# A transformer block with adaptive layer norm: turning rotated queries and keys by DMA instead of TensorE in 22 of 32 tiles

## The chip, the cores and the metric

The kernel runs as one program on one core of a Trainium2 chip. The metric is the device time of one execution in microseconds; the kernel before takes 1667.65 us (median of three runs, 1667.3 to 1667.76). All data is float32 unless said otherwise. Engines are called as in the profile: PE is TensorE's matrix multiplication and PEld its weight load, DVE is VectorE, ACT is ScalarE, POOL is GpSimd, SP is SyncE, which issues most of the DMAs.

## What is computed

The input x has 2 batches of 2048 tokens with 256 features. Six vectors per batch (`sa` to `gb`) come from a small conditioning matrix. Cut to what matters:

```python
h = layernorm(x) * (1 + ca) + sa
k = apply_rope(h @ Wk.T); v = h @ Wv.T            # one key and value head of 128
q = apply_rope(einsum('btd,hkd->bhtk', h, Wq))    # two query heads of 128
scores = einsum('bhtk,bsk->bhts', q, k) * 128 ** -0.5     # causal
x = x + ga * (softmax(scores) @ v ... @ Wo.T)
h = layernorm(x) * (1 + cb) + sb
x = x + gb * ffn(h)         # 8 experts, 256 -> 1024 -> 256, each token weighed by a gate

# apply_rope, on pairs of neighbouring features:
out = stack([x0 * cos - x1 * sin, x1 * cos + x0 * sin], axis=-1)
```

The gate gives a token to those experts alone whose softmax weight lies above a threshold of its own, so the experts work on lists of tokens.

## The kernel before

It has two parts. The **attention part** (function `attention`) goes over 32 tiles of 128 tokens, 16 of each batch. The **experts' part** (function `experts`) then goes over the eight experts' lists in items of 256 tokens, in loops whose counts are read from the data; its two products are L1202 (h) and L1193 (y). It begins when the attention part has ended, at about 488 us.

The 32 tiles are taken in groups, four tiles of batch 0, four of batch 1 and so on, at the end in twos and ones. A tile's place in this sequence is its rank r, 0 to 31; tiles 8 to 11, for example, are tiles 4 to 7 of batch 0. The function `tile_steps` writes down the steps of one tile:

- Load x (L448, SP), moments (L423, L425 on DVE; L429, L430 on POOL), normalised rows xn (L459, DVE or POOL), their transposes on PE (L468), hT with scale and shift (L476, L478), and the projection to queries, keys and values (L489, PE, 128x512 in PSUM). ACT copies v (L495).
- The rotation: L505 multiplies queries and key by the cosines and L513, in two instructions, the swapped pairs by the signed sines (both DVE, out of PSUM into tiles t); L522 adds the two products, on DVE or POOL.
- The rotated tile is 128 tokens by 3 x 128 features. `turn_rot` transposes its three blocks on PE into PSUM (L529), and `qT_out` copies them out with ACT: the key's block into kT, which holds all keys of a batch (L532), the queries' two blocks into qT, times the scale 128^-0.5 (L534).
- The scores (L545, PE) against all keys so far, at most 512 at a time, a causal mask on the last block (L549); `keep` copies them to SBUF and takes their maximum (L556, DVE, with a product by 1.0); L563, exp on ACT (L572), transposes of the weights (L618), their copy (L622), product with v (L628), output projection (L662), sum with x (L669), store (L678).
- Second layer norm (L685, L688), a split of the float32 rows into 16-bit halves on POOL (L695) and their store to a list of features (L702), the gate (L710 to L727), and for each group of tiles the places in the experts' lists, which POOL scatters (L826).

After the last tile, PE does two items of the first expert ahead (L975, L992), whose tokens were gathered from the features, transposed by DMA as 16-bit halves (L918) and joined by DVE (L924).

The order of the work is settled when the program is built, by the class `Plan`. Each step is added with an engine or a choice of engines, a cost for each in microseconds, steps that it comes after, buffers that it takes and gives back (`room` holds how many of each there are), a rank, and `late`, the time until its result is there once its engine is free. `Plan.run` goes through time: of the steps that are ready, whose engine is free and whose buffers are there, it takes the one of lowest rank, on the first of its engines that is free. Each engine then runs its instructions in exactly this order; a change of a cost or of a buffer's room can change the order on all engines. On the chip an instruction waits for semaphores of what it depends on.

## Time and profile before

| What | us |
|---|---|
| median of three runs | 1667.65 |
| the profiled execution | 1669.28 |
| its span, from first to last instruction | 1667.5 |
| PE busy, whole span | 1621.9 |
| start of the experts' first product L1202 | 488.39 |
| PE busy, 60 to 175 us (115 us) | 112.18 |
| DVE busy, 60 to 175 us | 90.27 |
| PE busy, 175 to 400 us (225 us) | 224.00 |
| DVE busy, 175 to 400 us | 139.62 |

A line of a group gives the source line, engine, operation, what it writes and reads, shape and count; then its busy time in us and the mean of one in ns; then how long the engine was idle just before such instructions, and what ended that. The busy time of PE counts each matrix multiplication to its modelled end, though the next has begun by then, so neighbours overlap. A line of a timeline begins with start and length in us. A line of the table by stage gives the stretch, its length, and the busy time of each engine with its number of instructions, then the granted clock of PE, the share of the DMA engines and GB/s.

### The profile page before, as it was taken

What the parts mean: (1) busy time and instruction counts of PE and PEld (TensorE: products, weight loads), DVE (VectorE), ACT (ScalarE), POOL (GpSimd) and SP (SyncE); (2) the same over time, 40 slices, a digit from 0 to 9 for tenths busy, and PEclk for the clock granted to TensorE, in tenths of its full rate; (3) what the DMA queues carried; (4) which work ended last, traced back from release to release, by engine and by line L of the source; (5) the groups of instructions that cost most, each with busy time, mean ns of one, the idle gap of its engine ahead of it and who ended that gap; (6) DMA issues with size and microseconds to landing.
All of it is one profiled execution on the core that took longest, in us unless ns stands there. A gap on an engine that the chain in (4) does not pass through costs nothing.

```text
span 1667.5 us, 26732 instructions
## 1 busy us (share of the span) xinstructions
PE 1621.9 (97%) x7666; PEld 1349.4 (81%) x7666; DVE 660.7 (40%) x2144; ACT 582.1 (35%) x1417; POOL 912.0 (55%) x1032
## 2 busy tenths in 40 slices
PE   8999999999989999999999999999999999999997
PEld 5666776777778888888888888888888888888886
DVE  6987666566532222223322322232232222222322
ACT  3555655555522222222222222222222222222222
POOL 5565334231127767647756765675776477634443
PEclk9999999999999999999999999999999999999999
DMA  5411000010033353335335333533533333433333
GB/s 181 149 39 36 23 30 26 17 39 14 14 87 57 62 115 60 62 57 109 56 65 108 57 59 58 108 57 59 108 57 59 57 58 58 69 57 57 64 57 48
DMA packets 165949, 106.35 MB, mean 64 GB/s; under 512 B 111040, under 2 KB 157248, under 8 KB 165760
## 3 DMA queue, kind: packets, MB, share of 16 engines
q0 software_dynamic: 41968, 46.83, 17.6%
q1 hardware_dynamic: 116048, 46.22, 12.1%
q10 hardware_dynamic: 7872, 12.58, 2.4%
q8 instruction: 26, 0.43, 0.1%
q14 instruction: 35, 0.29, 0.1%
HBM read 50.39 MB, written 31.86 MB: 49 GB/s over the span
## 4 chain that ended last, share of the span: by engine, by line
PE 67%; issue 1%; DMA 1%; another core or an unknown queue 1%; POOL 1%; POOLq 0%; DVE 0%; ACT 0%; SPq 0%; DVEq 0%; ACTq 0%
PE y L1193 33%; PE h L1202 33%; DMA list<-entry,place 0%; POOL out L1352 0%; DMA out<-yo,who 0%; ACT g L1228 0%; DMA xp<-xr 0%; DMA xr<-feats,at 0%; POOL list L1342 0%; POOL out L1385 0%; POOLq L1143 0%; DVE xT L1256 0%; DVE yb L1280 0%; DVE yo L1295 0%
## 5 line engine op out<-in xcount | busy, mean ns | idle before, releaser
L1193 PE MATMUL y<-w,g 128*128 128x256 f32 x2640 | 658.2, 381 | 15.3 <-ACT g L1228 10.4
L1202 PE MATMUL h<-xT,w 128*128 128x256 f32 (+1 forms) x2752 | 659.6, 373 | 4.7 <-DVEq L1306 4.7
L1228 ACT ACTIVATE g<-h,b_sb 128x256 f32<-128x256 f32 (+1 forms) x688 | 317.9, 465 | 860.9 <-PE h L1202 744.2
L1202 PEld LDWEIGHTS h<-xT,w 128*128 128x128 f32 x2752 | 515.0, 192 | 74.8 <-DVEq L1306 5.1
L1193 PEld LDWEIGHTS y<-w,g 128*128 128x128 f32 x2640 | 498.6, 190 | 86.0 <-ACT g L1228 11.9
L1352 POOL DMA_INDIRECT out<-yo,who x172 | 282.2, 1641 | 231.2 <-DVE yo L1295 178.2
L1256 DVE COPY xT<-xp 128x512 uint16<-128x512 uint16 x172 | 68.4, 439 | 647.3 <-PE h L1202 522.8
L1342 POOL DMA_INDIRECT list<-new,to x216 | 227.7, 1054 | 93.6 <-issue 75.3
L1318 POOL DMA_INDIRECT xr<-feats,at x172 | 175.0, 1017 | 100.5 <-POOL at L1363 70.5
L545 PE MATMUL psc<-kT,qT 128*128 128x512 f32 (+3 forms) x320 | 143.4, 534 | 0.0
L628 PE MATMUL pav<-pT,v 128*128 128x256 f32 x544 | 142.6, 384 | 0.0
L556 DVE TENSOR_SCALAR_CACHE_REDUCE s<-psc 128x512 f32<-128x512 f32 (+3 forms) x160 | 95.3, 605 | 62.5 <-PE psc L545 48.2
L628 PEld LDWEIGHTS pav<-pT,v 128*128 128x128 f32 x544 | 96.0, 190 | 29.7 <-issue 20.1
L1280 DVE TENSOR_TENSOR yb<-y,b_bc 128x256 f32<-128x256 f32 x165 | 62.6, 420 | 138.2 <-PE y L1193 134.4
L572 ACT ACTIVATE s<-s,nmx 128x512 f32<-128x512 f32 (+3 forms) x160 | 103.9, 651 | 36.9 <-DVE nmx L563 36.4
L622 ACT COPY pT<-ptr 128x512 f32<-128x512 f32 (+1 forms) x144 | 76.6, 564 | 51.7 <-PE pav L628 33.2
L826 POOL DMA_INDIRECT list<-entry,place x40 | 42.6, 1066 | 74.2 <-DVE place L823 43.4
L1271 DVE SCALAR_TENSOR_TENSOR gate<-gb_bc,mcur,part 128x256 f32<-128x256 f32 x172 | 75.8, 482 | 3.0
L618 PEld LDWEIGHTS ptr<-ident,s 128*128 128x128 f32 x544 | 63.4, 142 | 14.3 <-ACT s L572 4.5
L618 PE MATMUL ptr<-ident,s 128*128 128x128 f32 x544 | 72.5, 274 | 2.1 <-ACT s L572 1.9
L429 POOL TENSOR_SCALAR rstdf<-mvf 128x1 f32<-128x1 f32 x32 | 8.7, 272 | 113.5 <-DVE mvf L425 86.1
L1363 POOL COPY at<-sheet 128x2 int32 x85 | 61.2, 720 | 10.5 <-DMA xp<-xr 10.5
(165 smaller groups left out, 1104.8 us busy)
## 6 DMA issues: line engine op xcount, KB each, us to landing
w<-in_w ACTq DMA_DIRECT2D x12, 1024.0 KB
x<-in_x SPq DMA_DIRECT2D x32, 128.0 KB, 2.1
out<-x SPq DMA_DIRECT2D x32, 128.0 KB, 1.7
feats<-hp SPq DMA_DIRECT2D x32, 128.0 KB, 1.7
w<-in_w SPq DMA_DIRECT2D x4, 1024.0 KB, 9.1
list<-new,to POOLq DMA_INDIRECT x216
xr<-feats,at POOLq DMA_INDIRECT x172
out<-yo,who POOLq DMA_INDIRECT x172
```

What stands on the lines that cost most here:

```text
L545: nc.tensor.matmul(ps[:, :w], st["qT"][:, h, :], kT[:, ds(c * SC, w)], start=True, stop=not last)
L556: nc.vector.tensor_scalar(s[:, :w], st["sc", h, c][:, :w], 1.0, None, ALU.mult, ALU.max, accum_out=st["mx", h][:, c : c + 1],)
L572: nc.scalar.activation(s[:, :w], s[:, :w], AF.Exp, bias=st["nmx", h], accum_out=st["den"][:, h, c : c + 1],)
L618: nc.tensor.transpose(ptr[:, j, h, :], s[:, ds((c0 + j) * P % SC, P)], ident)
L622: nc.scalar.copy(pT[:, :m], st["ptr", c0][:, :m])
L628: nc.tensor.matmul(st["pav"][:, : NH * P], v[:, c0 + j, :], st["pT", c0][:, j].rearrange("p h t -> p (h t)"), start=(c0 + j == 0), stop=(c ...
L1193: last = pe.matmul(ys[c], gs[f % 4][:, ts(c, P)], weights[e][1][:, f, :], start=(f == 0), stop=(f == NF - 1),)
L1202: last = pe.matmul(hs[f % 4][:, :w], weights[e][0][:, k, ts(f, P)], xT[:, k, :w], start=(k == 0), stop=(k == KD - 1),)
L1228: act.activation(gs[f % 4][:, :w], hs[f % 4][:, :w], AF.Gelu_apprx_tanh, bias=b1_sb[:, at : at + 1],).then_inc(sem["act"], 1)
L1318: pool.indirect_dma_start(out=xr[:, ts(c, 2 * D)], out_offset=None, in_=feats, in_offset=bass.IndirectOffsetOnAxis(ap=at[:, c : c + 1], ax ...
L1342: pool.indirect_dma_start(out=lists[e], out_offset=bass.IndirectOffsetOnAxis(ap=to[:, j : j + 1], axis=0), in_=new[:, j, :], in_offset=Non ...
L1352: pool.indirect_dma_start(out=rows, out_offset=bass.IndirectOffsetOnAxis(ap=who[:, c : c + 1], axis=0), in_=yo[:, c, :], in_offset=None, b ...
```

## The change

In tiles 8 to 29 the three transposes on PE and the two copies on ACT are replaced by three steps. `rot_halves` (POOL) splits the rotated tile, 128x384 float32, into its low and its high 16-bit halves, 128x768. `turn_rot_halves` (SP) transposes these six blocks of 128x128 with one DMA from SBUF to SBUF. `join_rot` (DVE, or POOL if DVE isn't free in the plan) interleaves the halves again, into kT and into qT, with two copies. Tiles 0 to 7, 30 and 31 go on as before. Since a join doesn't multiply, the scale moves from `qT_out` to `keep`, for all tiles.

The rotary table holds each cosine and sine once instead of twice (and the sines without sign): L505 reads each value twice by a step of zero, and of the two instructions of L513 the first becomes a product by -1 and by the table in one instruction. The four loads of the table are 256 KB each instead of 512. The tiles t get buffers of their own (`t0` and `t1`, three each, in place of the shared name `big`), the second of which also holds the halves; `rpT` has two. In the plan, the cost of xn on POOL goes from 0.65 to 1.3.

```diff
-    room = {"ps": 6, "pav": 2, "x": 9, "s": 16, "pT": 3, "hx": 4, "hp": 3, "qT": 3, "big": 3, "xn": 3,
-            "hT": 2, "hT2": 2, "aT": 2, "g_sb": 1, "sign": 1, "size": 1, "ga": 1}
+    room = {"ps": 6, "pav": 2, "x": 9, "s": 16, "pT": 3, "hx": 4, "hp": 3, "qT": 3, "t0": 3, "t1": 3, "xn": 3,
+            "hT": 2, "hT2": 2, "rpT": 2, "aT": 2, "g_sb": 1, "sign": 1, "size": 1, "ga": 1}
...
-    rope_sb = const.tile([P, NT, 2, HS], F32, name="rope_sb")
+    rope_sb = const.tile([P, NT, 2, HS // 2], F32, name="rope_sb")
...
-        n_n = add(["DVE", "POOL"], [0.42, 0.65], xn, [n_n], take=["xn"])
+        n_n = add(["DVE", "POOL"], [0.42, 1.3], xn, [n_n], take=["xn"])
...
             if z == 0:
-                src = src.rearrange("p (h f) -> p h f", h=3)
                 nc.vector.tensor_tensor(
-                    dst, src, table.unsqueeze(1).to_broadcast([P, 3, HS]), ALU.mult
+                    d4, src,
+                    table.unsqueeze(1).unsqueeze(3).to_broadcast([P, 3, HS // 2, 2]), ALU.mult,
                 )
             else:
...
-                for y in range(2):
-                    nc.vector.tensor_tensor(
-                        d4[:, :, :, y], src[:, :, :, 1 - y],
-                        t4[:, :, y].unsqueeze(1).to_broadcast([P, 3, HS // 2]), ALU.mult,
-                    )
-
-        n_r0 = add("DVE", 0.6, lambda: rot(0), [n_q, l_rope[i // 4]], take=["big"])
-        n_r1 = add("DVE", 0.75, lambda: rot(1), [n_q, n_v, n_r0], give=["ps"])
+                t3 = table.unsqueeze(1).to_broadcast([P, 3, HS // 2])
+                nc.vector.scalar_tensor_tensor(
+                    d4[:, :, :, 0], src[:, :, :, 1], -1.0, t3, ALU.mult, ALU.mult
+                )
+                nc.vector.tensor_tensor(d4[:, :, :, 1], src[:, :, :, 0], t3, ALU.mult)
+
+        n_r0 = add("DVE", 0.6, lambda: rot(0), [n_q, l_rope[i // 4]], take=["t0"])
+        n_r1 = add("DVE", 0.75, lambda: rot(1), [n_q, n_v, n_r0], take=["t1"], give=["ps"])
         n_r = add(
             ["DVE", "POOL"], [0.58, 1.0],
             lambda eng: of[eng].tensor_tensor(st["t", 0], st["t", 0], st["t", 1], ALU.add),
-            [n_r0, n_r1],
+            [n_r0, n_r1], give=["t1"],
         )
...
-            nc.scalar.mul(st["qT"].rearrange("p h t -> p (h t)"), st["pr"][:, : NH * P], scale)
-
-        n_t = add("PE", 0.48, turn_rot, [n_r], take=["ps"], give=["big"])
-        n_k = add("ACT", 0.65, qT_out, [n_t], take=["qT"], give=["ps"])
+            nc.scalar.copy(st["qT"].rearrange("p h t -> p (h t)"), st["pr"][:, : NH * P])
+
+        def rot_halves():
+            st["rp"] = work([P, 2, 3 * HS], "t1", "_h" + u, U16)
+            nc.gpsimd.tensor_copy(
+                st["rp"],
+                st["t", 0].rearrange("p h f -> p (h f)").bitcast(U16).rearrange(
+                    "p (f two) -> p two f", two=2
+                ),
+            )
+
+        def turn_rot_halves():
+            st["rpT"] = work([P, 2 * 3, P], "rpT", u, U16)
+            nc.sync.dma_start_transpose(st["rpT"], st["rp"].rearrange("p two f -> p (two f)"))
+
+        def join_rot(eng):
+            src = st["rpT"].rearrange("p (two h) t -> p h t two", two=2)
+            of[eng].tensor_copy(
+                kT[:, ts(i, P)].bitcast(U16).rearrange("p (t two) -> p t two", two=2),
+                src[:, 2],
+            )
+            st["qT"] = work([P, NH, P], "qT", u)
+            of[eng].tensor_copy(
+                st["qT"].bitcast(U16).rearrange("p h (t two) -> p h t two", two=2),
+                src[:, :NH],
+            )
+
+        if 8.0 <= r < NTOK // P - 2:
+
+            n_t = add("POOL", 0.95, rot_halves, [n_r], take=["t1"], give=["t0"])
+            n_t = add("SP", 1.3, turn_rot_halves, [n_t], late=2.2, take=["rpT"], give=["t1"])
+            n_k = add(
+                ["DVE", "POOL"], [0.75, 1.1], join_rot, [n_t], take=["qT"], give=["rpT"]
+            )
+        else:
+            n_t = add("PE", 0.48, turn_rot, [n_r], take=["ps"], give=["t0"])
+            n_k = add("ACT", 0.65, qT_out, [n_t], take=["qT"], give=["ps"])
...
-                s[:, :w], st["sc", h, c][:, :w], 1.0, None, ALU.mult, ALU.max,
+                s[:, :w], st["sc", h, c][:, :w], scale, None, ALU.mult, ALU.max,
...
-    cos, sin = np.cos(angles), np.sin(angles)
-    both = np.stack([cos, cos], axis=-1), np.stack([-sin, sin], axis=-1)
-    return np.concatenate([a.reshape(T, HS) for a in both], axis=1).astype(np.float32)
+    return np.concatenate([np.cos(angles), np.sin(angles)], axis=1).astype(np.float32)
```

More of the change, by code (lines that the diff above doesn't have):

```diff
@@ L294, in attention @@
         load(rope_sb[:, ds(4 * q, 4)], rope.rearrange("(q n p) (z f) -> p q n z f", p=P, n=4, z=2)[:, q],
-             512, rank=first if q == 0 else q * 8 - 7.5)
+             256, rank=first if q == 0 else q * 8 - 7.5)
         for q in range(NT // 4)
@@ L501, in rot @@
             table = rope_sb[:, i, z, :]
-            src = st["pq"][:, : 3 * HS]
+            src = st["pq"][:, : 3 * HS].rearrange("p (h j two) -> p h j two", h=3, two=2)
+            d4 = dst.rearrange("p h (j two) -> p h j two", two=2)
             if z == 0:
-                src = src.rearrange("p (h f) -> p h f", h=3)
                 nc.vector.tensor_tensor(
-                    dst, src, table.unsqueeze(1).to_broadcast([P, 3, HS]), ALU.mult
-                )
-            else:
-                src = src.rearrange("p (h j two) -> p h j two", h=3, two=2)
-                d4 = dst.rearrange("p h (j two) -> p h j two", two=2)
-                t4 = table.rearrange("p (j two) -> p j two", two=2)
-                for y in range(2):
-                    nc.vector.tensor_tensor(
-                        d4[:, :, :, y], src[:, :, :, 1 - y],
-                        t4[:, :, y].unsqueeze(1).to_broadcast([P, 3, HS // 2]), ALU.mult,
-                    )
-        n_r0 = add("DVE", 0.6, lambda: rot(0), [n_q, l_rope[i // 4]], take=["big"])
-        n_r1 = add("DVE", 0.75, lambda: rot(1), [n_q, n_v, n_r0], give=["ps"])
+                    d4, src,
+                    table.unsqueeze(1).unsqueeze(3).to_broadcast([P, 3, HS // 2, 2]), ALU.mult,
+                )
+            else:
+                t3 = table.unsqueeze(1).to_broadcast([P, 3, HS // 2])
[5 more added lines that the diff above has]
+        n_r1 = add("DVE", 0.75, lambda: rot(1), [n_q, n_v, n_r0], take=["t1"], give=["ps"])
         n_r = add(
```

## The prediction

> **What bounds the kernel now.** I read the page first (busy time, then the chain), then busy times by stage, the groups of instructions of the first 470 us, PE's waits, and PE's timeline around the transposes. The page:

> ```profile
> PE 1621.9 (97%) x7666; PEld 1349.4 (81%) x7666; DVE 660.7 (40%) x2144; ACT 582.1 (35%) x1417; POOL 912.0 (55%) x1032
> PE y L1193 33%; PE h L1202 33%; DMA list<-entry,place 0%; POOL out L1352 0%; DMA out<-yo,who 0%; ACT g L1228 0%; DMA xp<-xr 0%; DMA xr<-feats,at 0%; POOL list L1342 0%; POOL out L1385 0%; POOLq L1143 0%; DVE xT L1256 0%; DVE yb L1280 0%; DVE yo L1295 0%
> ```

> TensorE is busy all the time. The chain names only the experts (L1193, L1202), which start at 488 us and which the diff leaves alone: every microsecond that the attention part ends earlier moves them as a block. So the question is what bounds the part before. By stage (us, PE, PEld, DVE, ACT, POOL busy):

> ```profile
> 60.00:175.00 115.00, 112.18 (x555) 78.54 (x554) 90.27 (x343) 64.88 (x191) 69.49 (x100) 1.00 0.14 41
> 175.00:400.00 225.00, 224.00 (x1090) 160.41 (x1089) 139.62 (x520) 130.38 (x359) 69.07 (x96) 1.00 0.09 26
> ```

> In the second stretch PE has no spare time and DVE is at 62%. In the first PE is at 98%, but DVE at 78% is the runner-up (from 60 to 100 us it has 36.61 of 40 us). What the steps cost:

> ```profile
> L529 PE MATMUL pr<-ident,t 128*128 128x128 f32 x96 | 15.3, 275 | 2.6 <-POOL t L522 2.6
> ...
> L532 ACT COPY kT<-pr 128x128 f32<-128x128 f32 x32 | 8.5, 267 | 19.8 <-PE pr L529 19.1 <-PE pf L866 0.8
> ...
> L534 ACT ACTIVATE qT<-pr 128x256 f32<-128x256 f32 x32 | 12.6, 394 | 0.0
> ```

> 275 ns is not what a transpose takes from PE, since neighbours overlap. Its real price is the distance between starts:

> ```profile
> 405.02 3.25 PE L618 MATMUL ptr<-ident,s 128*128 128x128 f32 x28
> 408.11 1.03 PE L628 MATMUL pav<-pT,v 128*128 128x256 f32 x4
> ```

> 28 transposes of the same shape hold PE from 405.02 to 408.11: 0.110 us each, 0.33 us for the three of a tile.

> [...]

> **The change, part by part.**
> *PE.* In tiles 8 to 29 (22 tiles) three transposes go: 22 x 0.33 = 7.3 us of PE's own time. Tiles 8 to 17 have them before 175 us (3.3 us), tiles 18 to 29 after (4.0 us). With them goes a wait of PE for the rotated tile (POOL t L522), 1.8 us at 112 us; the other one (0.8 us at 57 us) is of an earlier tile and stays. What PE meets next without it are the features' transposes (L710, which wait for DVE, 1.4 us from 60 to 400 us).
> *ACT.* 22 x (0.267 + 0.394) = 14.5 us of copies go. ACT is at 57% there: worth nothing by itself. One PSUM buffer of six per tile goes too, which lets PE run further ahead; I count nothing.
> *POOL.* New: the split, 128x768 uint16. Nearest row: L695, 128x512 in 613 ns, so 613 x 768/512 = 0.92 us, 22 x 0.92 = 20 us. In the order in which the changed kernel issues, POOL also gets 13 of the 22 joins; a join is 256 + 512 elements, by the same row 0.31 + 0.61 = 0.92 us, 12 us; it loses 3 additions (1.01) and 5 of L459 (1.27), 9 us. Net +23 us, on an engine with 60% in the first stretch and 31% in the second: hidden.
> *DVE.* 9 joins: the same pattern as L924, 128x512 in 0.42 us, and half of that to all of it for the 256; I take 0.26: 0.68 x 9 = 6.1 us. Plus 3 additions (0.556) and 5 of L459 (0.47): 4.0 us. Net +10 us. The rotation's new form (one product by -1, the table repeated by a zero step) has the same elements; no row shows it. Ends: 0 to +0.1 us in each of 32 tiles; I take 0. The scale moves into L556, which multiplied by 1.0 before: nothing.
> *SP and the transfer.* 22 more issues. The row for it, of eight blocks where the new one has six:

> ```profile
> L918 SPq DMA_TRANSPOSE sign_p<-g_sb_r x2: 1231/1292/1352, 342.0 to 352.5; - x2
> ...
> DMA to landing us min/median/max: 3.0/3.1/3.1
> ```

> 22 x 1.29 = 28 us of SP's sequencer, mostly idle there; the landing is between 3.1 x 6/8 = 2.3 and 3.1 us, I take 3.1. Most new issues stand right behind a store of features (L702, waiting for POOL) and ahead of a store of results (L678, waiting for DVE); behind them wait loads of x, which run tiles ahead. DMA engines are at 9 to 14%.
> *Latency.* From the added tile to keys that can be scored it took 0.33 + 0.27 + 0.27 + 0.39, about 1.2 us. It will take 0.92 + 3.1 + 0.92 plus three handovers of 0.1, 5.2 us: 4 us more. The cover for that is the distance from a tile's projection to its first score. The tightest is tile 8:

> ```profile
> 62.67 1.88 PE L489 MATMUL pq<-wqkv_sb,hT 128*128 128x512 f32 x4
> ...
> 68.70 0.82 PE L529 MATMUL pr<-ident,t 128*128 128x128 f32 x6
> ...
> 74.89 1.02 PE L545 MATMUL psc<-kT,qT 128*128 128x512 f32 x2
> ```

> Its transposes start at 69.0 us, so 5.9 us lie between them and the score, 4.7 us spare. In the changed order the PE work between projection and score, added up with the pitches, is 12.6 us for tile 8, 13.0 and 13.7 us for tiles 14 and 15, 15 to 71 us for the others. So 4 us fit, barely in three tiles: a late landing there costs PE up to 2 us each. Tiles 30 and 31, with nothing behind them, stay on PE.
> *Order.* The planner deals all work anew. It draws projections and rotations forward (tile 31's by some 70 us), so about four more tiles' rotations (4 x 1.3 = 5 us of DVE), and most of the +10 us, fall before 175 us: DVE goes from 90 to about 102 of 115 us, 89%. There PE and DVE will stop each other more. Of the 3.3 + 1.8 us that go there I let 3.0 count; of the 4.0 us after, all.
> *Start.* The first part of the rotary table is 256 KB instead of 512 KB. PE's first wait is for another load (wm, 6.5 us), issued before it: nothing.

> Sum: 3.0 + 4.0 = 7.0 us. The profiled execution took 1669.3 us, its span 1667.5; it would become 1662.3 and 1660.5. The median of the runs is 1667.65, so I predict 1660.6.

> **The rivals.** *Everything counts* (chance 0.12): PE keeps all 7.3 + 1.8 us, and the freed PSUM buffers remove a few of the short gaps, 1 to 4 us: 1654 to 1658. For it: the larger distances. Against: DVE at 89%.
> *VectorE takes over before 175 us* (0.21): the gain there is lost and DVE's extra work pushes by up to 3 us; only the 4.0 us of the second stretch stay, 1663.7 to 1667. For it: 36.61 of 40 us at 60 to 100 us. Against: there its waits for scores (L556, 48.2 us in all to 460 us) still leave room.
> *Joins hold up their engines* (0.12), slower. Joins stand in DVE's and POOL's fixed order; behind one that waits for its landing stand the rstd of other tiles (L429, L430), then their normalised rows, then PE. If each of the 22 costs PE 0.6 us, that is 13.2 us against 7.0 gained: 1673.9. It decides above 0.32 us a tile on the mean. Against: the planner books 1.3 + 2.2 = 3.5 us for what I measure as at most 3.1, so joins should come after their landings.
> *It doesn't do what it says*: excluded; 30 instead of 96 transposes of rotated tiles are issued.

> **How the numbers follow.** The likeliest case has 0.55 (1658 to 1664), with the rivals 0.12, 0.21 and 0.12. A measurement of this kernel tells 0.2%, 3.3 us, from no change: faster is below 1664.3, slower above 1671.0. Faster: 0.55 + 0.12 + 0.03 of the VectorE case = 0.70; slower: 0.10; the rest 0.20. The range of 8 in 10 leaves out most of the slower case and the best of the better one: 1656 to 1668.5.

> **What would show it.** Right: the start of the experts' first long row of h (L1202, 488.39 us now) comes 7 us earlier; PE's time from 175 to 400 us falls by the pitch of the transposes, and PE waits for no join. Wrong: PE waiting for kT or qT in tiles 8, 14 and 15; DVE above 95% from 60 to 175 us; POOL's L429 waiting behind a join; landings above 3.5 us.

## The result, and the profile after

The changed kernel takes 1680.39 us (median of six runs, 1676.69 to 1685.88); the kernel before took 1667.7 us beside it (six runs, 1664.71 to 1673.84). The ratio is 1.0067, with an interval of 1.0048 to 1.0085: slower by 12.7 us, where 7 us less had been forecast. The profiled execution of the changed kernel took 1685.88 us, the longest of its six.

The attention part got shorter, as forecast, though by less. Its stages (us; busy time of PE, PEld, DVE, ACT, POOL, each with its count; then PE's clock, DMA share, GB/s) in the changed kernel:

```profile
60.00:175.00 115.00, 111.91 (x531) 77.00 (x530) 99.08 (x358) 61.53 (x173) 81.29 (x117) 1.00 0.25 63
175.00:400.00 225.00, 222.64 (x1065) 158.07 (x1064) 142.05 (x530) 127.36 (x340) 79.71 (x116) 1.00 0.14 35
```

DVE is at 99 us of 115 (90 before), POOL 22 us busier over both stretches, PE a little less busy. The new work, in the groups of instructions of the attention part and in the view of the tile `rpT`:

```profile
L536 POOL COPY t_h<-t 128x768 uint16<-128x768 uint16 x22 | 18.6, 847 | 4.3 <-DVE t L520 4.1
...
L554 POOL COPY qT<-rpT 128x512 uint16<-128x512 uint16 x13 | 9.0, 694 | 15.2 <-PE psc L580 10.6 <-PE pc L836 4.6
...
L549 POOL COPY kT<-rpT 128x256 uint16<-128x256 uint16 x13 | 5.4, 417 | 4.5 <-DMA rpT<-t_h 4.5
```

```profile
L545 SPq DMA_TRANSPOSE rpT<-t_h x22: 1210/1217/1682, 69.6 to 312.0; - x22
...
DMA to landing us min/median/max: 2.7/2.8/3.1
```

The split takes 0.85 us, a join 1.1 us on POOL, a landing 2.8 us. One figure in the second group matters later: POOL's joins stood still for 10.6 us until PE had read an older tile of queries. PE's waits in the attention part, after:

```profile
PE ph L741 <- DVE hx L719: 2.6, 6, 1.0
...
PE psc L576 <- POOL qT L554: 0.7, 1, 0.7
```

PE waits once for a join (0.7 us, at about 361 us), and more often than before for the features' rows (1.5 us in three waits there). Its last product of the attention part (`pya`) starts at 480.57 us, 2.78 us earlier than the 483.35 of before. PE's timeline at the seam (start, duration, line, idle before):

```profile
479.49 1.46 PE L1023 MATMUL pya<-w,s_g 128*128 128x256 f32 x6
486.47 3.74 PE L1233 MATMUL h<-xT,w 128*128 128x256 f32 x8 [5.52 <-issue]
```

So the experts start at 486.47 instead of 488.39 us. The wait at this seam grew by 0.85 us (before: 4.67 us, put down to DVE), so of the 2.78 us only 1.92 arrive there. From there to the end it takes 1196.8 us instead of 1179.1: the loss of 17.7 us lies wholly in a part that the diff doesn't touch, in which PE issues the same 5392 products. PE's waits in it, before and then after:

```profile
PE y L1193 <- ACT g L1228: 10.4, 8, 2.4
PE y L1193 <- issue: 4.6, 5, 2.1
PE y L1193 <- DVE yb L1280: 0.2, 1, 0.2
```

```profile
PE y L1224 <- ACT g L1259: 12.5, 15, 2.4
PE y L1224 <- issue: 6.9, 6, 2.2
PE h L1233 <- issue: 6.0, 4, 5.3
```

The last line is new. "issue" means that no semaphore explains the idle time. The longest case, in the timeline after:

```profile
1053.51 1.03 PE L1233 MATMUL h<-xT,w 128*128 128x256 f32 x4
1054.37 2.75 PE L1224 MATMUL y<-w,g 128*128 128x256 f32 x12
1054.97 0.38 ACTq L1268 DMA_DIRECT2D w<-in_w  x1
1062.45 3.78 PE L1233 MATMUL h<-xT,w 128*128 128x256 f32 x8 [5.32 <-issue]
```

It falls where PE goes from the fourth expert to the fifth: the line of ACT is the load of weights that ACT issues as it begins the fifth (L1268, one such load at the beginning of each of the first six experts). All that the next item waits for was there: the join of `xT` (L1287) was done at 1055.4 us, and the fifth expert's weights had been asked for at 763.9 us. This change of experts is a special one. The last item of an expert's list is a half item of 128 tokens if the list fills an odd number of 128-token tiles, and its code stands between the expert's loop and the next expert's. PE's products show a half item at the end of seven of the eight experts, as here at the third's (h is 128x128 instead of 128x256):

```profile
889.90 1.50 PE L1233 MATMUL h<-xT,w 128*128 128x128 f32 x12
```

The fourth expert alone has none, so there PE jumps over the half item's code. Behind the pause, eight products take 3.78 us, where four take 1.03 otherwise: the clock is halved (the granted clock is 0.50 from 1062.4 to 1066.3 us). The stretch of 1050 to 1080 us, before and then after:

```profile
1050.00:1080.00 30.00, 30.00 (x140) 26.21 (x139) 8.81 (x24) 7.43 (x16) 18.54 (x22) 1.00 0.58 124
```

```profile
1050.00:1080.00 30.00, 24.68 (x105) 21.05 (x104) 5.85 (x17) 5.60 (x12) 14.90 (x18) 0.89 0.54 115
```

140 products became 105. Over the whole experts' part, the distances between starts of PE's products exceed the usual 0.216 us by 40.5 us in sum after and 23.8 us before. Of that, products at halved clock account for 7.8 and 4.1 us, and pauses for the other 32.7 and 19.8 us. So 16.6 us of the 17.7 are explained, 12.9 by pauses and 3.7 by the clock. The pause at 1057 us and the slow products behind it are 7.7 us of this; the rest are shorter waits and the slow products behind them, of kinds that the kernel before has too; this execution is the longest of the six.

What was PE waiting for? The list of DMA queues has a kind that no line of the kernel issues; the page after, and the same list for the stretch from 1057 to 1062 us:

```profile
q8 instruction: 25, 0.41, 0.1%
```

```profile
q8 instruction: 1, 0.02, 1.3%
```

The times of these packets behind 484 us:

| kernel | PE's blocks of instructions, start in us |
|---|---|
| before | 602.6, 758.7, 894.2, 1054.6, 1176.0, 1342.1, 1547.3, 1648.2 |
| after | 491.3, **758.6, 792.7, 1059.6, 1091.8**, 1358.0, **1563.4, 1595.1**, 1685.2 |

Before, one comes with each of the seven half items, and one 2.8 us after the change from the fourth expert to the fifth. After, there are three pairs, 32 to 34 us apart (bold), and each stands across a change of experts, at 765, 1057 to 1062 and 1568 us: by that assumption the blocks' edges lie elsewhere in the experts' code. An expert's code of PE is 258 instructions long in the compiled program, nearly one such block, so an edge would fall at much the same point of every expert's code. The change took 135 instructions from PE ahead of this code (66 transposes are 132), and 44 copies from ACT. The place of an engine's loops is, in what follows, their position in the compiled program modulo 256, up to a constant that is the same for all kernels: 86 before and 207 after for PE, 81 and 37 for ACT. Where in this count a block begins isn't known; only the differences between places are used.

**Theory**: the change gains in the attention part what the traces show, and loses more because the loops of the experts' part slid to a bad place. **Rival**: the DMA transposes, or the smaller rotary table in memory, leave something behind that slows the experts.

### The profile page after: what moved, and what is told of

The parts are those of the page before. It is cut to its first block, busy times and chain, and to the rows that moved or that the text cites. A ratio compares the mean times of both kernels' runs of the same rounds, so it can differ in the third digit from the quotient of the medians.

```text
span 1683.3 us, 26660 instructions
## 1 busy us (share of the span) xinstructions
PE 1625.4 (97%) x7600; PEld 1348.3 (80%) x7600; DVE 665.3 (40%) x2169; ACT 572.8 (34%) x1374; POOL 931.2 (55%) x1072
## 4 chain that ended last, share of the span: by engine, by line
PE 68%; issue 1%; another core or an unknown queue 0%; ACT 0%; DMA 0%; POOLq 0%; DVE 0%; POOL 0%; DVEq 0%; ACTq 0%
PE h L1233 34%; PE y L1224 34%; ACT g L1259 0%; DMA out<-yo,who 0%; POOLq L1174 0%; DVE yo L1326 0%; DVE xT L955 0%; POOL out L1383 0%; DVE yb L1311 0%; DVEq L1523 0%; POOLq L1476 0%; POOLq L1383 0%; DVE who L1317 0%; POOLq L1478 0%
## 5 line engine op out<-in xcount | busy, mean ns | idle before, releaser
L1383 POOL DMA_INDIRECT out<-yo,who x172 | 282.9, 1645 | 244.9 <-DVE yo L1326 191.9
L1287 DVE COPY xT<-xp 128x512 uint16<-128x512 uint16 x172 | 67.7, 435 | 682.5 <-PE h L1233 637.1
L1373 POOL DMA_INDIRECT list<-new,to x216 | 223.0, 1032 | 94.4 <-issue 75.2
L576 PEld LDWEIGHTS psc<-kT,qT 128*128 128x128 f32 x320 | 57.2, 190 | 19.8 <-issue 7.4
```

The lines of the kernel that those rows point to most:

```text
L576: nc.tensor.matmul(ps[:, :w], st["qT"][:, h, :], kT[:, ds(c * SC, w)], start=True, stop=not last)
L1373: pool.indirect_dma_start(out=lists[e], out_offset=bass.IndirectOffsetOnAxis(ap=to[:, j : j + 1], axis=0), in_=new[:, j, :], in_offset=Non ...
L1383: pool.indirect_dma_start(out=rows, out_offset=bass.IndirectOffsetOnAxis(ap=who[:, c : c + 1], axis=0), in_=yo[:, c, :], in_offset=None, b ...
```

## Experiments: the place of the loops

The kernel before, run beside these kernels, took 1645.0, 1670.4, 1664.1 and 1645.0 us on the chips of the four sets of runs below; a ratio is to the kernel before of its own set. A filler is an instruction that does nothing:

```python
nc.tensor.nop(nofuse=True, hint="pad")      # or nc.scalar
```

**The changed kernel again** (no edit).

> The changed kernel once more, unaltered, for the spread of its experts' part. Its profiled execution had the first expert product at 486.5 us and 1196.8 us from there to the end, against 488.4 and 1179.1 us before. Place of the code (theory 1): again about 486.5 us, then 1188 to 1197 us, total 1677 to 1686. Chance alone (rival: single long waits that fall on any execution): the part after 487 us comes out anywhere from 1179 to 1197 us.

1651.07 us, ratio 1.0044 (1.0028 to 1.0061). The loss is there on another chip. In the profiled execution PE made no pause above 0.7 us in the experts' part, and it took 1643.91; the three others took 1650.99 to 1654.36. By these times the pause comes in most executions, not in each. The packets of the profiled one differ from those of the execution above, though the program is the same: the pairs stand at 600.2 and 631.3, 877.0 and 909.1, 1521.2 and 1553.2 us, and none at the change to the fifth expert. What all traces at this place share is smaller: the wait at the seam takes 5.4 to 5.9 us and is put down to "issue" in all five traces of kernels at place 207, with a later pause or without, and takes 4.3 to 4.7 us in the 13 others.

**The changed kernel, loops at the old places.**

```diff
 # by_feature, ahead of PE's first product
+for _ in range(135):
+    nc.tensor.nop(nofuse=True, hint="pad")
 # behind ACT's silu
+for _ in range(44):
+    nc.scalar.nop(nofuse=True, hint="pad")
```

> The changed kernel with 135 empty instructions on PE before its first product and 44 on ACT after its first activation, where both engines wait anyway. With them the experts' loops of PE and ACT stand at the same index in these engines' instruction streams as in the kernel before. Theory 1 [...]: the experts' part falls from about 1192 to about 1179 us, total 1665 to 1668. Rival 2 (addresses in DRAM moved by the smaller rotary table, or something the DMA transposes leave behind): it stays at 1190 to 1197 us, total 1677 to 1684.

1646.16 us, ratio 1.0006 (0.9997 to 1.0014). The first product came at 10.78 instead of 6.80 us, so the fillers cost 4.0 us; in spite of that it is 4.9 us shorter than the changed kernel without them. No pause of PE in the experts' part exceeds 0.6 us.

**The kernel before, loops at the changed kernel's places.**

```diff
+121 fillers on PE ahead of its first product
+52 fillers on ACT behind silu, 5 behind each of the 32 copies of v
```

> The kernel before with 121 empty instructions on PE and 212 on ACT (52 at the start, 5 after each copy of v), which put the experts' loops of these two engines at the index of the changed kernel, counted modulo 256. Nothing of the change is in it. Theory 1: the experts' part rises from 1179 to 1188 to 1197 us, the attention part stays within 1.5 us, total 1677 to 1686. Rival 2: the experts' part stays at 1179 us, total 1667 to 1670.

1659.69 us, ratio 1.0090 (1.0073 to 1.0107). Nothing of the change is in it. 3.2 us are the later start (first product at 9.76 us); most of the rest is one pause of 6.4 us between the same two items as in the changed kernel, and the slow products behind it (seven in 3.35 us; in the changed kernel it was eight in 3.78, at a clock of 0.50). PE's waits in its experts' part (from 495 us), its timeline, and the instruction packets between 1040.4 and 1047.2 us:

```profile
PE h L1212 <- issue: 6.8, 3, 6.4
```

```profile
1037.98 2.75 PE L1203 MATMUL y<-w,g 128*128 128x256 f32 x12
1047.16 3.35 PE L1212 MATMUL h<-xT,w 128*128 128x256 f32 x7 [6.42 <-issue]
```

```profile
q8 instruction: 1, 0.02, 0.9%
```

Again one packet of 16 KB lies inside the pause (from 1044.3 us), and the pairs are back: 752.4 and 784.4, 1044.3 and 1077.2, 1537.0 and 1568.6 us.

**The changed kernel without the DMA turn.** All tiles turn on PE; table, rotation and moved scale stay.

```diff
-        if 8.0 <= r < NTOK // P - 2:
+        if False:
```

> The changed kernel with all 32 tiles turned by PE as before; the halved table, the product by -1, the moved scale and the plan's costs stay. If the DMA transposes make the attention part's 2 us and more: the first expert product comes at 488 to 491 us. If the transposes are worth nothing and the rest of the edit brought it: 486 to 487 us. The experts' part is not forecast, since its loops stand at a third place.

1644.02 us, ratio 0.9994 (0.9985 to 1.0003). Its loops stand at places 84 and 72, near the old ones, and its packets come as in the kernel before. The table, the rotation and the moved scale can't be the cause. Attention's last product starts at 482.14 us here and at 478.71 in the changed kernel on the same chip: the turn gains 3.4 us there.

**Fillers ahead of everything.**

```diff
 # attention(), first lines
+135 fillers on PE, 44 on ACT
```

> The changed kernel with 135 instructions that do nothing on TensorE and 44 on ScalarE, now ahead of everything else, where both engines wait for their first data anyway (PE's first product comes at 6.5 us; 135 x 30 ns = 4.0 us), so that the experts' loops of these two engines stand at the same places (modulo 256 instructions) as in the kernel before. Theory (place of the loops costs the experts' time, the transposes themselves gain): first product at 6.5 to 6.9 us, end of attention's PE work 3 to 4 us ahead of the kernel before, experts' part as short as before (within 1 us), so 3 to 4 us under the kernel before: ratio 0.998, and no gap of PE above 1 us in the experts' part. Rival (something that the DMA transposes or the smaller table leave behind slows the experts): 0.4 to 0.7% over the kernel before, ratio 1.004 to 1.007, with gaps of several us.

Ratio 0.9993 (0.9979 to 1.0008). Half a miss: the first product still came at 10.78 us. Fillers at the start aren't free, since 75 of them delayed nothing in another run (6.41 us), 121 delayed by 3.2 and 135 by 4.2 us: about 0.07 us each beyond the first ones. The experts' part shows no pause for "issue" above 0.7 us.

**One engine at a time**, in the kernel before:

```diff
+121 fillers on PE alone, ahead of everything      # before_pe_moved
+212 fillers on ACT alone, ahead of everything     # before_act_moved
```

> The kernel before with 121 instructions that do nothing on TensorE alone, ahead of everything else: its experts' loops stand where they stand in the changed kernel (207 modulo 256), ScalarE's stay. Theory with TensorE's fetch as the cause: the stall of 5 to 7 us at about 1040 us and a clock halved behind it come back, experts' part 5 to 11 us longer, ratio 1.004 to 1.007. Theory with ScalarE's fetch as the cause: nothing, ratio 1.000, no gap above 1 us. Both engines together gave 1.009.

> The kernel before with 212 instructions that do nothing on ScalarE alone, ahead of everything else: its experts' loops stand where they stand in the changed kernel (37 modulo 256), TensorE's stay. Theory with ScalarE's fetch as a cause: TensorE's y waits for g (1 to 2.5 us each, some six of them), experts' part 3 to 8 us longer, ratio 1.002 to 1.005. If TensorE's place is the only cause: ratio 1.000.

Ratios 1.0093 (1.0068 to 1.0118) and 1.0031 (1.0021 to 1.0041). PE's place makes the large loss, with a pause of 5.1 us for "issue" that ends at 1059.9 us, between those same items, and a packet from 1057.2 us inside it; its later start is 3.2 us, or 0.19%. For ACT the first product was late as well (11.17 us, 4.6 us more, 0.28% of the time), which accounts for its ratio: no loss by ACT's place is shown.

**Which place.** Fillers behind the products of the projection (L489), where nothing is delayed:

```diff
 # qkv(), behind each of its 64 products
+4 fillers: 256                              # before_pe_256, place 86 again
+2 fillers, 1 behind the last seven: 121     # before_pe_spread, place 207
+1 filler: 64                                # before_pe_64, place 150
```

> The kernel before with 256 filler instructions on TensorE, four behind each product of the projection: everything behind them moves on by 256 instructions, so the experts' loops keep their place modulo 256 (86) and are further from the beginning. Theory (the place within a block of 256 instructions counts): as the kernel before, ratio 1.000 within 0.002, no gap of 5 us. Rivals (the distance from the beginning, the number of instructions, or the fillers themselves count): as bad as the 121 fillers or worse, ratio 1.007 to 1.010 or above.

> The kernel before with 121 filler instructions on TensorE, two behind each product of the projection (one behind the last seven), so that nothing is delayed at the start and the experts' loops stand at 207 modulo 256, as in the changed kernel. Theory (place): attention as in the kernel before, a gap of 5 to 7 us at about 1040 us and an experts' part longer by 8 to 15 us, ratio 1.006 to 1.010. Rival (the delayed start had caused the loss in the run with the same fillers ahead): ratio 1.000.

> The kernel before with 64 filler instructions on TensorE, one behind each product of the projection: the experts' loops stand at 150 modulo 256, between the good place (86) and the bad one (207). Theory (place): a value of its own, most likely between the two, ratio 0.999 to 1.008; which one isn't predicted. Rival (the number of added instructions counts): half of the loss of 121, ratio 1.004 to 1.005.

Ratios 0.9990 (0.9984 to 0.9997), 1.0048 (1.0035 to 1.0061) and 0.9994 (0.9986 to 1.0002). 256 fillers cost nothing, 121 cost 7.9 us (0.0048 of 1645): neither their number nor the distance from the beginning counts, but the place within 256. Place 150 is as good as 86. With 121 the blocks came in pairs again (602.2 and 633.6, 879.3 and 911.3, 1523.4 and 1554.9 us), with the others one by one. Four of its six executions took 1653.8 to 1655.3 us and one 1647.9; the profiled one took 1646.27 and shows no pause, and no packet at the change to the fifth expert. So of the forecast pause only the time is shown there, not the row; and pairs alone don't make a pause. The queue also confirms whose blocks these are: with 256 fillers on PE it has 27 instead of 26.

```profile
q8 instruction: 27, 0.44, 0.1%
```

**The changed kernel at the good place, nothing delayed.**

```diff
 # qkv(), behind each product
+2 fillers, 3 behind the first seven: 135    # after_spread, after_pe_only
 # behind each copy of v
+1 filler, 2 behind the first twelve: 44     # after_spread
```

> The changed kernel once more with its experts' loops of TensorE and ScalarE at the places of the kernel before (86 and 81), the 135 and 44 instructions that do nothing now spread behind the products of the projection (two behind each, 0.43 us long) and the copies of v, so that the first product isn't delayed as it was by 4 us where they all stood ahead of it. Theory: first product at 6.5 to 6.9 us, end of attention's PE work at 478.5 to 480.6 us as in the changed kernel, experts' part within 1 us of the kernel before, hence 3 to 4 us under the kernel before: ratio 0.9978 (0.997 to 0.999). If the fillers delay TensorE here as well, or the experts' part stays long for another reason: ratio 1.000 or above.

> The changed kernel with TensorE's loops alone at the place of the kernel before (135 spread fillers), ScalarE's at 37 where the change put them. With both placed the ratio was 0.9968; ScalarE's place alone cost the kernel before 0.3%. If the two add up: ratio 0.999 to 1.000. If TensorE's place is all that counts in this order: 0.997.

1657.98 us, ratio 0.9968 (0.9959 to 0.9977), and 1641.40 us, ratio 0.9977 (0.9968 to 0.9986). With its loops in place the change is faster than the kernel before, by 5.3 and 3.8 us; PE alone is enough. PE's waits in the experts' part of after_spread:

```profile
PE y L1231 <- ACT g L1266: 8.3, 8, 1.7
PE y L1231 <- issue: 1.3, 2, 0.6
```

The line "PE h <- issue" is gone. All DMA transposes and the smaller table are in these two kernels, so the rival, something that they leave behind, is refuted.

## Experiments: what the attention part gains

All four have PE's loops at place 86 and ACT's at 81, by fillers. The end of the attention part scatters: its last product starts at 478.7 to 480.6 us in four traces of the changed kernel's order in which nothing was delayed, and at 481.0 to 483.4 us in four of the kernel before. So a difference of less than about 2 us between two traces shows nothing by itself, and `late_tiles` and `no_dma_turn` ran on other chips than the rest.

**The turn in part of the tiles.**

```diff
-        if 8.0 <= r < NTOK // P - 2:
+        if 18.0 <= r < NTOK // P - 2:     # late_tiles: 12 of 22
+        if 8.0 <= r < 18.0:               # early_tiles: 10 of 22
```

> The changed kernel with the DMA turn in tiles 18 to 29 alone (12 of 22 tiles; the others as before), loops of TensorE and ScalarE placed as in the kernel before by 75 and 25 instructions that do nothing ahead of everything else. Removed from TensorE's stream: 12 x 0.33 = 4.0 us. If the missing 4 us of the gain were lost before 175 us, where VectorE is busy for 99 of 115 us, the whole 4.0 us stay here and the end of attention's PE work comes 3.5 to 4.0 us ahead of the kernel without the turn: ratio 0.9977. If every tile returns about half of its gain in small waits wherever it stands: 1.7 to 2.2 us, ratio 0.9988. If the joins' buffers (a query tile that waits for an older one to be read) cost what is lost: 0 to 1.5 us, ratio 0.9995.

> The changed kernel with the DMA turn in tiles 8 to 17 alone (10 of 22), loops placed as in the kernel before by spread fillers. Removed from TensorE's stream: 10 x 0.33 = 3.3 us, and the wait of 1.8 us at 112 us. With all of the turn the end of attention's PE work came at 478.7 us, without it at 482.1, with tiles 18 to 29 alone at 481.8. If most of the gain is made in the early tiles and the late ones return theirs in waits: 478.5 to 479.5 us here, ratio 0.998. If both parts gain about half and only the run of the late tiles happened to lose it: 480.0 to 480.8 us, ratio 0.9990.

Attention's last product starts at 481.81 us with the late tiles alone (ratio 0.9992, 0.9980 to 1.0004) and at 478.46 with the early ones alone (ratio 0.9977, 0.9967 to 0.9987), against 482.14 without the turn and 478.95 with all of it (after_spread). The early tiles gain 3.7 us, the late ones within the scatter nothing: the reverse of what the prediction let count. (By the ratios the late ones would add 1.5 us to the early ones, and the intervals of the early and the late tiles alone overlap; the split is read from the traces.) PE's waits in late_tiles, up to 481 us:

```profile
PE ph L745 <- DVE hx L723: 4.3, 7, 1.6
PE ph L745 <- DVE s L591: 0.9, 2, 0.5
PE psc L580 <- POOL qT L558: 0.7, 1, 0.7
```

Without the turn the first of these lines says 0.7 us: PE comes to the features' transposes, and DVE hasn't normalised their rows yet. Behind 175 us PE's waits of more than 0.15 us add up to 5.9 us here and to 2.4 us without the turn, so 3.5 of the 4.0 us are given back there. The forecast that named the joins' buffers had the number, not the cause: PE waited 0.7 us for a join.

**What a transpose is worth.** Without the DMA turn, tiles 8 to 29 turn their rows on PE twice, in an unchanged order.

```diff
-            for h in (2, 0, 1):
+            for h in (2, 0, 1) * (2 if 8.0 <= r < NTOK // P - 2 else 1):
```

> The changed kernel without the DMA turn, in which tiles 8 to 29 turn their rotated rows on TensorE twice over, into the same place (66 transposes more, the same result; the planner's costs, so the order of everything, unchanged; fillers place the loops as in the kernel before). What 22 x 0.33 = 7.3 us of TensorE's stream are worth there with nothing else moved. If the stream is the bound and a transpose's pitch is its price, the end of attention's PE work goes from 482.1 to 489.4 us and the time up by 7.3 us: ratio 1.0044. If part of a transposes' pitch fits into gaps that stand there anyway, 3.5 us: 485.6 us, ratio 1.002; then the change could never have gained 7.

1667.20 us, ratio 1.0018 (1.0009 to 1.0028), 3 us over the kernel before and 4 over no_dma_turn's ratio. Since the order is the same, the same products can be compared one by one; the lead (minus) or lag of double_turn against no_dma_turn, which ran on another chip (its start came 0.5 us earlier, and the lead had grown to 1.88 us by 27 us, ahead of all extra transposes):

| tile's transposes at, us | lag ahead of them | lag behind them |
|---|---|---|
| 73.2 | -1.88 | -1.56 |
| 86.6 | -1.73 | -1.41 |
| 94.0 | -1.73 | -1.41 |
| 111.2 | -1.74 | -1.41 |
| 150.2 | -0.49 | -0.17 |
| 190.3 | +0.44 | +0.77 |
| 319.1 | +2.31 | +2.64 |
| at the end | +2.97 | |

Each extra set of three costs 0.33 us where it stands. But between the sets lag is given back (-1.41 to -1.73 from 86.6 to 94.0): PE's next wait is that much shorter. In sum 7.3 us of work moved the end by 4.85 us, from -1.88 to +2.97: neither all, as the first forecast had it, nor half, as the second, but two thirds. (The ratio is the second's, 1.002, but the early start is in it.)

**More buffers for turned queries.**

```diff
-"qT": 3
+"qT": 5
```

> The changed kernel with five buffers for a turned tile of queries instead of three, loops placed as in the kernel before by spread fillers. In the changed kernel joins on GpSimd wait 10.6 us (twice, 6.8 us the longest) for an older tile's buffer, and TensorE's scores then wait for that join 0.7 us, its weight loads 1.5 us. If the buffers cost part of the missing 4 us, that wait is gone and the end of attention's PE work comes 1 to 1.5 us earlier, at 477.3 to 477.8 us, ratio 0.997. If what TensorE loses is VectorE's lateness with the features' rows, or just a different deal of the planner: no change beyond 0.5 us, or a loss.

1656.17 us, ratio 0.9956 (0.9940 to 0.9972), the fastest kernel of all. Attention ends at 477.38 us, 1.6 us before after_spread on the same chip, and PE's matrix unit no longer waits for a join:

```profile
PEld psc L583 <- POOL qT L561: 0.4, 2, 0.2
```

The 1.6 us lie within the scatter, part of them may be the planner's new deal, and the two intervals of the whole time overlap: that the buffers bring it is not shown. One POOL join still stood behind PE for 10.6 us, but no product waited for it.

## Why the prediction was wrong, point by point

*"... the experts (L1193, L1202), which start at 488 us and which the diff leaves alone: every microsecond that the attention part ends earlier moves them as a block."* This is the step that failed. The source of the experts' part is unchanged, its place in the compiled program isn't. The block moved 1.9 us ahead and grew by 17.7 us. In its place the runs show: PE's loops at place 207 of 256 cost the kernel before 0.5% with nothing delayed; put back to 86 the changed kernel goes from ratios of 1.0044 and 1.0067 to 0.9968 and 0.9977. That is 0.6 to 1.0% (0.6 on one chip, after_again against after_placed less its late start), and the two runs of the kernel before with a late start lose about 0.7% by the place; why the place costs more in one kernel or chip than in another isn't shown.

*The rivals.* None named this. The slower one, joins that hold up their engines, would have given 1673.9 us by PE's waits in the attention part. The time went above it by another way, and PE's one wait for a join was 0.7 us: that rival is refuted though the sign was its own.

*PE: 22 x 0.33 = 7.3 us.* The price held to the hundredth (double_turn). What it moves was mis-sized: 4.85 us there, since PE's other waits take the rest. The change itself gained 2.8 us on the first chip and 3.2 to 3.4 us against no_dma_turn, 4.8 with more buffers.

*"Of the 3.3 + 1.8 us that go there I let 3.0 count; of the 4.0 us after, all."* The early 3.0 came out as 3.7 (early_tiles), the late 4.0 as nothing (late_tiles). DVE's busy share was taken as the sign of where gains are lost; it is highest where the gain was full. What lost the late gain were PE's waits for single late rows, in a stretch where DVE is at 63%.

*DVE to about 102 us, POOL net +23 us:* 99.1, and 81.3 - 69.5 + 79.7 - 69.1 = 22.4 us. Right.

*Split, join, landing:* 0.92, 0.92 and 3.1 us forecast, 0.85, 1.11 on POOL and 2.8 measured; on DVE 0.29 + 0.42 in the median, 0.68 forecast. Right in kind. PE met no late landing in tiles 8, 14 and 15.

*Start and rotation's new form at nothing:* no_dma_turn holds both and has ratio 0.9994. Right within 0.1%.

*The buffer.* The prediction counted handovers and landing into the join's latency and not the room for its result: three `qT` tiles, each held until its tile's last score. One wait of PE, 0.7 us, is shown for it.

The sum at a fixed place would have been 3.8 to 5.3 us instead of 7.0; the range, 1656.0 to 1668.5, would have held it.

What stays open. All three profiled pauses stand at the change from the fourth expert to the fifth, the one at which PE jumps over a half item. Counted along PE's queue, the packet in the pause is the 21st in the changed kernel (1059.6 us) and the 22nd in the kernel before with 121 fillers (1044.3 and 1057.2 us). In the two traces at place 207 without a pause the packet of the same number had come at 909.1 and 911.3 us, long before the jump. So PE paused where the block wasn't there yet. This is inferred from five traces: no run gave the fourth expert a half item or took another's away. Why the same program gets the block early in one execution and late in another isn't known.

What sets the length of the pause is open too. The packet started 2.3 to 3.6 us after PE's last product had ended, and PE went on 1.8 to 1.9 us after the packet's end. Between that product and the packet the share of the DMA engines was 0.87 to 1.03, since ACT had just asked for weights. The packet may have stood behind them; no run tells that apart.

That the halved clock comes with a pause is the plainer part: from the seam to 1640 us the changed kernel's trace has five stretches of granted clock 0.50, of 3.4 to 6.8 us, and each begins 1.1 to 3.5 us after the start of a pause. But three of these pauses were of 1.7 to 2.4 us only, and a pause of 2.2 us that ended at 621.6 us brought none. Which pause brings it isn't shown.

## What to carry to other kernels

An edit that adds or removes instructions ahead of a loop moves the loop in the compiled program: place 207 instead of 86 cost 0.5 to 1% here, more than the edit was worth. So compare variants with the loops held at the same place (256 fillers behind products that start 0.43 us apart cost nothing here, ratio 0.9990), and when a stage that wasn't touched changes its time, look at the times of the instruction queue's packets too, and at the jumps in the code. And a microsecond of a busy engine was not worth a microsecond here, since its next waits took a part: 7.3 us of transposes moved the end by 4.85 us. So count the waits behind it.

## What was not expected of the hardware

- A pause of PE of 5.1 to 6.4 us, with one 16 KB packet of instructions of 1.0 us inside it, where PE jumps over a piece of code; with the loops at place 207 some blocks come in pairs 31 to 34 us apart, at 86 or 150 none do.
- The same program at the bad place is slow in most executions and not in all: 1643.91 against 1650.99 to 1654.36 us on one chip. Its blocks of instructions don't come at the same points in each: the 21st at 1059.6 us in one, at 909.1 in another.
- Fillers on PE cost about 0.07 us each ahead of its first product, beyond the first 75 or so, and nothing behind products that start 0.43 us apart, even four of them (ratio 0.9990).
- The 128x768 transpose of 16-bit halves landed 2.7 to 3.1 us from its issue, which takes 1.22 us of SP.
